# A decoder block with routed experts on one core: the rows of the attention operands are filled straight from SBUF tiles instead of through DRAM

## The chip, the core and the metric

The kernel runs on one core of a Trainium2 chip. The metric is the device time of one execution in microseconds (us). Three runs of the kernel before gave 652.01, 650.23 and 651.17 us, a median of 651.17 us.

## The reference, cut to what matters

The inputs are `x` and `ctx`, both of 32 sequences x 128 tokens x 128 features in float32. There are 16 heads of 8 features each.

```
x = layernorm(x + attn(x, x, causal), ln1)
x = layernorm(x + attn(x, ctx), ln2)
x = layernorm(x + moe(x), ln3)            # 8 experts, 128 -> 512 -> 128, the two best of each token
attn: Q, K, V = linear maps; scores = Q K^T / sqrt(8) by head; softmax; times V; output map
```

## The kernel before, in words

**Tiles and stages.** The 32 sequences go through in 8 groups of 4 (`G = 4`). Each group has a self-attention item ("s") and a cross-attention item ("c"), taken in the order s0, s1, s2, c0, s3, c1 and so on. An s item has 3 steps and a c item 4, so there are 56 steps. In each step TensorE computes scores with queries on the partitions (`scores_q`), VectorE takes each query's maximum (`maximum`, L995), and 3 steps later TensorE computes the same scores with keys on the partitions (`scores_k`), now with the maximum subtracted, and ScalarE takes the exponential (L1448). After the attention of all groups the tokens go through the experts in 71 blocks (L1680 to L1772).

**How a score is computed.** The products are in bfloat16, and an fp32 value is the sum of three bfloat16 parts. `parts` (L856) makes them for the queries ("q") or keys ("k") of one item, 32 times in all: one projection on TensorE (L788) gives 128 features x 512 tokens; ScalarE rounds it to part 1 (L864); VectorE takes the remainder (L868); GpSimd rounds that to part 2 (L872) and takes what is left as part 3 (L875); for the first queries VectorE does these two. The parts lie in a tile `p3`, of which there are 3. The operand of the scores is another tile `at` (`qk` in the profile; 3 for queries, 3 for keys): partition `8a + t` holds, for eight column blocks i (one for each pair of heads), term t of one feature. Terms 0 to 5 are six products of parts (`terms`), so that one matmul over 64 partitions sums them. On the query side, terms 6 and 7 carry the negated maximum, as a high and a low bfloat16 part; on the key side these rows hold a constant selector, `sel`.

**How the rows are filled.** The rows of `at` mix features of all heads, so the parts go through DRAM. The whole `p3` is stored to a DRAM tile `pd` (L885, 384 KB; for the first queries and keys part by part, L880), and six transfers of 128 KB read it back in the order that `at` wants (L901). On the query side the rows of the maximum must be zero while `scores_q` runs: when a query tile is used again, two transfers copy zeros from a DRAM tile `zero_d` (L896).

**How the maxima reach their rows.** `transposed_maxima` (L998) splits the maxima on GpSimd into high and low parts (L1008, L1009), transposes them on TensorE (L1016), copies them out on ScalarE (L1023) into `nmT` with 32 partitions, and two transfers spread the 16 high and the 16 low rows into rows 6 and 7 of each eight (L1029).

**What sets the order.** `Plan` (L172) simulates the engines and queues by listed durations, latencies and priorities, and writes out one fixed order for each engine; buffers are given out by the same simulation, from the first task that names a buffer until the last one that names it has ended. On the chip each engine and queue runs its list in order and waits by semaphores. SP's queue issues nearly all transfers, ACT's queue some weights and the rows of the first keys. The rows of an item may not be filled earlier than 5 steps ahead of its first step (`LEAD`, L1413 to L1415).

Of the kernel before, what the change touches and what calls it, by code (L numbers as in the profile page):

```python
# [10 lines left out]
BF16 = mybir.dt.bfloat16  # L11
# [6 lines left out]
P = 128  # L18
H = 16
HD = 8  # L20
E = 8
# [315 lines left out]
def kernel(  # L337
# [67 lines left out]
    sel = sb([P, 8], "sel")  # L405
    zero_d = dram.tile([16, 8, G * P], BF16, name="zero_d")
    maskq = sb([P, HALF], "maskq", BF16)
# [73 lines left out]
    def c_sel():  # L481

        nc.vector.tensor_scalar(ti[:, 2:3], ti[:, 0:1], 7, None, ALU.bitwise_and)
        nc.vector.tensor_scalar(ti[:, 3:4], ti[:, 0:1], 56, None, ALU.bitwise_and)
        nc.vector.tensor_copy(tf[:, 0:2], ti[:, 2:4])
        nc.vector.tensor_scalar(tf[:, 0:1], tf[:, 0:1], 6.0, ONES16, ALU.is_ge, ALU.mult)
        nc.vector.tensor_scalar(tf[:, 2:10], tf[:, 64:72], 8.0, None, ALU.mult)
        nc.vector.tensor_scalar(sel, tf[:, 2:10], tf[:, 1:2], tf[:, 0:1], ALU.is_equal, ALU.mult)
# [44 lines left out]
    def colsrc(src):  # L533
        return src.rearrange("(p o) -> p o", o=1)

    raw = {}
    t_raw = {}
    for n, w, prio, q in (
        ("wqs", sa_wq, -30, "ACT"), ("wks", sa_wk, -29, "ACT"), ("wvs", sa_wv, -26, "ACT"), ("wkc", ca_wk, -12, "SP"),
        ("wos", sa_wo, -16, "SP"), ("wvc", ca_wv, -11, "SP"), ("wqc", ca_wq, -13, "SP"), ("woc", ca_wo, -5, "SP"),  # L540
    ):
        raw[n] = spare[:, 0:P] if n == "wqc" else sb([P, P], n)
        t_raw[n] = load(raw[n], w, prio, q)
# [3 lines left out]
    for n, src, prio, q in (  # L547
        ("bqs", sa_bq, -28, "ACT"), ("bks", sa_bk, -27, "ACT"), ("bvs", sa_bv, -15.5, "SP"), ("g1", ln1_g, -12.9, "SP"),
        ("b1", ln1_b, -12.8, "SP"), ("bqc", ca_bq, -12.7, "SP"), ("bkc", ca_bk, -11.9, "SP"), ("bvc", ca_bv, -5, "SP"),
        ("g2", ln2_g, 0, "SP"), ("b2", ln2_b, 0, "SP"),  # L550
    ):
        cols[n] = sb([P, 1], "col_" + n)
        t_col[n] = load(cols[n], colsrc(src), prio, q)
    rws = {}
    t_row = {}
    for i, (n, src, w) in enumerate((
# [8 lines left out]

    wp = {n: raw[n] for n in ("wqs", "wks", "wkc")}
    t_wp = {n: t_raw[n] for n in wp}
    wp["wqc"] = sb([P, P], "wqcp")
    t_wqc = t_wp["wqc"] = early(
        "DVE", 0.3, -5, lambda: nc.vector.tensor_scalar(wp["wqc"], raw["wqc"], cols["g1"], None, ALU.mult),  # L570
        [t_raw["wqc"], t_col["g1"]],
    )
    bqc = sb([P, 1], "bqc")

    def pe(dur, prio, fn, deps, bufs, mode="128x128"):
# [3 lines left out]
    t = pe(  # L579
        0.3, -4, lambda b=b_q: nc.tensor.matmul(b.at[:, 0:1], lhsT=raw["wqc"], rhs=cols["b1"], start=True, stop=True),  # L580
        [t_raw["wqc"], t_col["b1"]], [b_q],
    )
# [207 lines left out]
    def prepare(kind, gi):  # L790
# [13 lines left out]
        def copied(b=bank):  # L804
# [10 lines left out]
        it.K, it.t_K, it.t_pK = parts(  # L815
            wp["wk" + n], cols["bk" + n], xT, [t, t_wp["wk" + n], t_col["bk" + n]], t0 - 4.45, (1, 2, 1, 2, 3, 1), f"k{kind}{gi}"
        )
# [38 lines left out]
    def parts(w, b, xT, deps, prio, terms, name):  # L856


        bank, p3, r1, at = Buf(s_ps), Buf(s_p3), Buf(s_r1), Buf(s_q if name[0] == "q" else s_kk)
        pd = dram.tile([3, P, G * P], BF16, name="pd_" + name)  # L860
        t1 = pe(1.12, prio, lambda: project(bank.at, w, xT.at), deps, [bank, xT, p3])
# [15 lines left out]
        soon = name in ("qs0", "ks0")  # L877
        if soon:
            t6 = it_store[name] = [
                add("SP", 0.5, -24 + 0.1 * k, lambda k=k: nc.sync.dma_start(out=pd[k], in_=p3.at[:, k, :]), [t_], [p3], lat=2.4)  # L880
                for k, t_ in enumerate((t2, t4, t5))
            ]
        else:
# [5 lines left out]
        q = "ACT" if name == "ks0" else "SP"  # L889
        dq = nc.scalar if q == "ACT" else nc.sync  # L890
# [7 lines left out]
        for t, k in enumerate(terms):  # L898

            def rows(t=t, k=k):  # L900
                dq.dma_start(out=at.at[t::8], in_=pd[k - 1].rearrange("(i a) n -> a i n", i=8))  # L901

            t7.append(
                add(q, 0.66 if q == "SP" else 0.85, (-23 + 0.1 * k if soon else prio + 0.37) + 0.01 * t, rows, [t6[k - 1], *cleared], [at], lat=3.6)
            )
        return at, t7, t5
# [91 lines left out]
    def transposed_maxima(tl, ti_, nm, deps):  # L998
# [5 lines left out]
        def split():  # L1004
            src = nm.at[:, 0 : 16 * two].rearrange("p (h j r a) -> p a j h r", h=2, j=2, r=4)
            for a in range(two):
                top, low = [nmx.at[:, a, k].rearrange("p j (h r) -> p j h r", h=2) for k in range(2)]
                nc.gpsimd.tensor_copy(top, src[:, a])  # L1008
                nc.gpsimd.tensor_tensor(low, src[:, a], top, ALU.subtract)  # L1009
# [3 lines left out]
        def tr():  # L1013
            b16 = bank.at.bitcast(BF16)
            for a in range(two):
                nc.tensor.transpose(  # L1016
                    b16[0:32, a * P : (a + 1) * P], nmx.at[:, a].rearrange("p k j c -> p (k j c)"), ident16
                )
# [7 lines left out]
        def spread():  # L1026
            c0 = P * tl[2] if tl[0] == "c" else 0 if two == 2 else 2 * P + P * tl[2]
            for k in range(2):
                nc.sync.dma_start(  # L1029
                    out=it.Q.at[6 + k :: 8, :, c0 : c0 + P * two],  # L1030
                    in_=bc(nmT.at[16 * k : 16 * k + 16, 0 : P * two], 1, 8),
                )

        it.nmt[tl] = add("SP", 1.3, ti_ - 18.37, spread, [t], [nmT, it.Q], lat=3.2)

# [838 lines left out]
```

## Time and profile before

| | us |
|---|---|
| median of three runs | 651.17 (650.23 to 652.01) |
| profiled execution, its own time | 654.44 |
| its span in the profile | 652.4 |
| PE (TensorE matmuls) busy | 481.2 (74%) |
| DVE (VectorE) busy | 360.5 (55%) |
| POOL (GpSimd) busy | 331.8 (51%) |
| ACT (ScalarE) busy | 315.0 (48%) |

The span is the time from the first to the last instruction that the profile shows; 654.44 - 652.4 = 2.0 us lie around it. The shares are averages over stages that differ: the filling of the pipeline, the steps of attention, and the expert blocks. The transfers moved 100.07 MB, a mean of 153 GB/s.

### The profile page before, as it was taken

Reading aid. Unit: us, or ns where it says so; the run is one execution under the profiler, and the core shown is the slowest. Engines: PE = TensorE matmul, PEld = TensorE weight load, DVE = VectorE, ACT = ScalarE, POOL = GpSimd, SP = SyncE. Lnnn points to the kernel's source line nnn. Section 1 sums busy time; section 2 is a strip of 40 time slices with the busy share of each in tenths; the row PEclk is TensorE's granted clock in tenths of the full one; section 3 lists DMA queues with packets and bytes.
Section 4 is the critical chain, followed back from the end, with each engine's and each line's share of the span. In section 5 each row is a group of like instructions: output and inputs, shape, how many; then the busy total and the mean of one; then the engine's idle time right before and its main releaser. Section 6 shows DMA issues by size and latency. Waiting matters only on the chain.

```text
span 652.4 us, 23363 instructions
## 1 busy us (share of the span) xinstructions
PE 481.2 (74%) x8571; PEld 370.6 (57%) x8571; DVE 360.5 (55%) x995; ACT 315.0 (48%) x719; POOL 331.8 (51%) x570
## 2 busy tenths in 40 slices
PE   6557688887788788898787845678848899696760
PEld 4234465564655554656565723577748788586750
DVE  5477436766678576786748747113602224635527
ACT  3214254565455654556563532545525567565630
POOL 4623114452357457367583765445365334657473
PEclk9567779988899989899899865689968999987975
DMA  5566776546664654745442134344448657665422
GB/s 156 123 203 174 200 201 181 174 146 199 173 168 118 191 153 136 210 122 168 145 147 87 32 110 118 103 137 137 133 136 246 182 173 229 191 191 153 150 76 64
DMA packets 118719, 100.07 MB, mean 153 GB/s; under 512 B 25931, under 2 KB 105967, under 8 KB 118144
## 3 DMA queue, kind: packets, MB, share of 16 engines
q1 hardware_dynamic: 107888, 84.69, 45.5%
q0 software_dynamic: 4320, 8.47, 3.8%
q10 hardware_dynamic: 6400, 5.45, 2.8%
q8 instruction: 69, 1.13, 0.8%
q14 instruction: 42, 0.34, 0.2%
HBM read 68.39 MB, written 26.42 MB: 145 GB/s over the span
## 4 chain that ended last, share of the span: by engine, by line
PE 37%; DVE 16%; issue 13%; POOL 9%; SPq 8%; DMA 8%; ACT 4%; another core or an unknown queue 3%; DVEq 1%; ACTq 0%; POOLq 0%
PE ps L935 12%; PE ps L1723 8%; PE ps L1745 8%; DVE nm L995 6%; SPq L901 4%; DMA qk<-nmT 3%; PE ps L788 2%; SPq L1029 2%; ACT pr L1448 2%; DVE y L1802 2%; POOL rs L1141 1%; PE ps L1705 1%; PE ps L782 1%; POOL res_d L1767 1%
## 5 line engine op out<-in xcount | busy, mean ns | idle before, releaser
L995 DVE TENSOR_REDUCE nm<-ps 128x8 f32<-128x1024 f32 (+1 forms) x112 | 133.1, 1219 | 43.9 <-PE ps L935 35.8
L1448 ACT ACTIVATE pr<-ps 128x1024 f32<-128x1024 f32 x112 | 110.9, 1023 | 86.6 <-PE ps L935 75.2
L935 PE MATMUL ps<-qk,qk 64*64 64x128 bf16 (+2 forms) x3072 | 99.1, 228 | 49.5 <-DVE nm L995 12.0
L935 PEld LDWEIGHTS <-qk 64*64 64x64 bf16 (+1 forms) x3072 | 66.3, 113 | 90.8 <-issue 36.4
L1767 POOL DMA_INDIRECT res_d<-o,id x71 | 70.0, 985 | 82.3 <-DVE o L1762 37.6
L1336 POOL DMA_INDIRECT rows_d<-y,rid x64 | 64.9, 1014 | 40.9 <-issue 17.2
L935 PE MATMUL ps<-pr,v 64*32 64x64 f32 (+2 forms) x3072 | 77.7, 277 | 7.4 <-issue 7.2
L935 PEld LDWEIGHTS ps<-pr,v 64*32 64x32 f32 (+1 forms) x3072 | 61.2, 115 | 24.1 <-issue 17.4
L1745 PE MATMUL ps<-wall,qk 128*128 x336 | 50.4, 298 | 18.6 <-ACT qk L1737 10.2
L1737 ACT ACTIVATE qk<-ps,b1c 128x128 f32<-128x128 f32 x168 | 48.1, 378 | 28.9 <-PE ps L1723 17.7
L1745 PEld LDWEIGHTS ps<-wall,qk 128*128 128x128 f32 x336 | 44.5, 207 | 23.4 <-ACT qk L1737 11.9
L1008 POOL CAST nmx<-nm 128x16 bf16<-128x16 f32 x64 | 12.6, 196 | 82.5 <-DVE nm L995 81.9
L1723 PE MATMUL ps<-bx,qk 128*128 128x128 f32 x336 | 47.7, 290 | 3.8 <-ACT bx L1710 3.8
L1737 ACT ACTIVATE k<-ps,b1c 128x128 f32<-128x128 f32 x116 | 33.2, 378 | 30.9 <-PE ps L1705 9.2
L1755 DVE TENSOR_SCALAR id<-xT,tab_e 128x1 int32<-128x1 f32 x47 | 12.8, 273 | 62.5 <-SPq L1640 28.8
L1723 PEld LDWEIGHTS ps<-bx,qk 128*128 128x128 f32 x336 | 44.1, 205 | 4.6 <-ACT bx L1710 4.0
L1095 DVE STREAM_TRANSPOSE u<-ps 128x512 f32<-128x512 f32 x32 | 21.8, 701 | 41.6 <-PE ps L935 40.5
L1762 DVE TENSOR_TENSOR o<-ps,b2r 128x128 f32<-128x128 f32 x71 | 20.1, 290 | 43.9 <-PE ps L1745 23.1
L1723 PE MATMUL ps<-bx,w 128*128 128x128 f32 x232 | 35.6, 306 | 10.6 <-ACT bx L1710 8.5
L1710 ACT ACTIVATE bx<-ps,col_b,col_g 128x128 f32<-128x128 f32 x71 | 33.0, 473 | 19.2 <-remote 9.2
L1723 PEld LDWEIGHTS ps<-bx,w 128*128 128x128 f32 x232 | 32.6, 217 | 12.1 <-ACT bx L1710 9.2
L1168 ACT ACTIVATE y<-y,rs 128x128 f32<-128x128 f32 x58 | 25.0, 491 | 29.8 <-POOL rs L1142 29.8
(269 smaller groups left out, 888.5 us busy)
## 6 DMA issues: line engine op xcount, KB each, us to landing
qk<-in_L_xattn_e_w_dram SPq DMA_DIRECT2D x42, 256.0 KB
w<-in_L_xattn_e_w_dram SPq DMA_DIRECT2D x29, 256.0 KB
qk<-pd_qs SPq DMA_DIRECT2D x48, 128.0 KB
qk<-pd_kc SPq DMA_DIRECT2D x48, 128.0 KB
qk<-pd_qc SPq DMA_DIRECT2D x48, 128.0 KB
qk<-pd_ks SPq DMA_DIRECT2D x42, 128.0 KB
qk<-zero_d SPq DMA_DIRECT2D x28, 128.0 KB
pr<-res_d ACTq DMA_DIRECT2D x7, 512.0 KB
```

Of the source, the lines that this page charges most:

```text
L901: dq.dma_start(out=at.at[t::8], in_=pd[k - 1].rearrange("(i a) n -> a i n", i=8))
L935: nc.tensor.matmul(out_, lhsT=lhsT, rhs=rhs, start=start, stop=stop, skip_group_check=True)
L995: lambda: nc.vector.tensor_reduce(dst(), src(), AX.X, ALU.max, negate=True), [dep], [pair, nm, turn],
L1095: t = add("DVE", dve(512), prio, lambda: nc.vector.transpose(u1.at, bank.at), [dep], [bank, u1])
L1168: lambda i=i: nc.scalar.activation(dst(i), src(i), AF.Identity, bias=rs.at[:, 1, i : i + 1], scale=rs.at[:, 0, i : i + 1],),
L1336: nc.gpsimd.indirect_dma_start(out=rows_d[:, :], out_offset=bass.IndirectOffsetOnAxis(ap=rid.at[:, i, k : k + 1], axis=0), in_=y.at[:, i, ...
L1448: lambda kp=kp, prb=prb, h=h: nc.scalar.activation(prb.at[:, 8 * h : 8 * h + 8, :].rearrange("p h q -> p (h q)"), kp.at.rearrange("p b n - ...
L1710: lambda: nc.scalar.activation(xT.at[:, 0:P], bt.at[:, 0:P], AF.Identity, bias=cols["b2"], scale=cols["g2"]),
L1723: nc.tensor.matmul(p1.at[:, c * P : (c + 1) * P], lhsT=w1.at[:, c, :], rhs=xT.at[:, 0:P], start=True, stop=True)
L1737: nc.scalar.activation(h.at[:, c, :], p1.at[:, c * P : (c + 1) * P], AF.Gelu, bias=b1c[:, bass.ds(w["act"] + c, 1)],)
L1745: nc.tensor.matmul(p2.at[:, 0:P], lhsT=h.at[:, c, :], rhs=flat[:, bass.ds(w["pe"] + c * P, P)], start=c == 0, stop=c == NFC - 1,)
L1767: nc.gpsimd.indirect_dma_start(out=res_d[:, :], out_offset=bass.IndirectOffsetOnAxis(ap=idb.at[:, 0:1], axis=0), in_=o.at, in_offset=None, ...
```

## The change: what it does

Three edits belong together.

1. The columns of the query and key weights (and the biases) are permuted once, so that feature 8a + i of a projection is what feature 16i + a was. Then the eight partitions 8a to 8a + 7 of a part are the eight column blocks of row a, and `at.at[t::8]` can be filled by one transfer from `p3.at[:, k, :]`, SBUF to SBUF. The stores to `pd` and the tile `pd` go. A row's transfer waits for its own part alone. `p3` is now named by the row transfers, so it is held until they have landed. The permutation is four VectorE copies of 128x128 float32; the raw weights lie in the memory of expert 5's second matrix until then.
2. The two rows of the maximum are terms 3 and 7 in place of 6 and 7. The high and low parts alternate in `nmx`, so that one transfer spreads all 32 rows of `nmT` to `at[3::4]`.
3. For the same reason one transfer of zeros to `at[3::4]` takes the place of two; `zero_d` has 32 rows of 8 KB.

The listed latency of a row transfer is 2.6 where it was 3.6, that of the spread 2.4 where it was 3.2. The loads that may not overtake the first fill (`begun`) wait in the plan for the row transfers instead of the stores.

```diff
+    for n, prio in (("wqs", -29.5), ("wks", -28.5), ("wkc", -5.1), ("wqc", -5.2)):
+        t_wp[n] = permuted(n, prio)      # early("DVE", 0.3, prio, tensor_copy(out_, byhead(raw[n])))
...
-            wp["wk" + n], cols["bk" + n], xT, [...], t0 - 4.45, (1, 2, 1, 2, 3, 1), f"k{kind}{gi}"
+            wp["wk" + n], cols["bk" + n], xT, [...], t0 - 4.45, (3, 2, 1, 0, 1, 2, 1, 0), f"k{kind}{gi}"
...
-            wp["wq" + n], b, xT, [t_xT, t_wp["wq" + n], t_b], prio, (1, 1, 2, 2, 1, 3), f"q{n}{gi}"
+            wp["wq" + n], b, xT, [t_xT, t_wp["wq" + n], t_b], prio, (1, 1, 1, 0, 2, 2, 3, 0), f"q{n}{gi}"
...
-        pd = dram.tile([3, P, G * P], BF16, name="pd_" + name)
...
-            t6 = [add(
-                "SP", 0.6, prio + -1.05, lambda: nc.sync.dma_start(out=pd.rearrange("k p n -> p k n"), in_=p3.at), [t5], [p3], lat=2.8
-            )] * 3
...
-        for t in (6, 7) if again else ():
-                add(q, 0.66, prio + 0.4, lambda t=t, dq=dq: dq.dma_start(out=at.at[t::8], in_=zero_d), [t4, t_zero, *cleared], [at], lat=3.0)
+        if again:
+                    q, 0.6, prio + 0.4,
+                    lambda: dq.dma_start(out=at.at[3::4].rearrange("a i n -> a (i n)"), in_=zero_d), [t4, t_zero, *cleared],
...
-                dq.dma_start(out=at.at[t::8], in_=pd[k - 1].rearrange("(i a) n -> a i n", i=8))
-                add(q, 0.66 ..., (-23 + 0.1 * k if soon else prio + 0.37) + 0.01 * t, rows, [t6[k - 1], *cleared], [at], lat=3.6)
+                    dq.dma_start(out=at.at[t::8], in_=p3.at[:, k, :])
+                    add(q, 0.6, (-23 + 0.1 * k if soon else prio + 0.37) + 0.01 * t, rows, [t_, *cleared], [p3, at], lat=2.6)
+                if soon:
+                    it_store.setdefault(name, []).append(t7[-1])
...
-            for k in range(2):
-                nc.sync.dma_start(
-                    out=it.Q.at[6 + k :: 8, :, c0 : c0 + P * two],
-                    in_=bc(nmT.at[16 * k : 16 * k + 16, 0 : P * two], 1, 8),
-                )
-        it.nmt[tl] = add("SP", 1.3, ti_ - 18.37, spread, [t], [nmT, it.Q], lat=3.2)
+            nc.sync.dma_start(out=it.Q.at[3::4, :, c0 : c0 + P * two], in_=bc(nmT.at[:, 0 : P * two], 1, 8))
+        it.nmt[tl] = add("SP", 0.65, ti_ - 18.37, spread, [t], [nmT, it.Q], lat=2.4)
```

## Rows read from the trace of the kernel before

**Rows 1.** Busy time of each engine (with its number of instructions), the granted TensorE clock as a share of full speed, the mean busy share of the 16 DMA engines and GB/s, in five stretches of the span.

```profile
0.00:30.00 30.00, 17.98 (x174) 10.40 (x174) 14.38 (x37) 9.08 (x14) 17.99 (x41) 0.81 0.58 147
30.00:60.00 30.00, 17.56 (x362) 9.86 (x362) 24.02 (x50) 7.29 (x11) 6.33 (x18) 0.63 0.60 173
...
210.00:240.00 30.00, 23.24 (x649) 16.69 (x649) 19.95 (x58) 17.42 (x30) 16.25 (x32) 0.94 0.71 202
360.00:400.00 40.00, 24.32 (x283) 17.71 (x283) 27.57 (x114) 13.67 (x31) 24.81 (x50) 0.71 0.30 90
...
420.00:652.00 232.00, 168.22 (x1289) 156.46 (x1289) 90.78 (x344) 119.36 (x390) 119.68 (x143) 0.88 0.54 158
```

**Rows 2.** The chain of work that ended last, over the whole span, by engine ("SPq" is SP issuing transfers, "DMA" a transfer under way).

```profile
PE 37%; DVE 16%; issue 13%; POOL 9%; SPq 8%; DMA 8%; ACT 4%; another core or an unknown queue 3%; DVEq 1%; ACTq 0%; POOLq 0%
```

**Rows 3.** What PE waited for from 60 to 385 us: total us, times, longest.

```profile
PE ps L935 <- issue: 17.0, 19, 4.2
PE ps L935 <- DMA qk<-nmT: 8.8, 6, 2.8
PE ps L935 <- DVE nm L995: 6.4, 15, 0.9
PE ps L935 <- ACT pr L1448: 6.2, 12, 1.0
...
PE ps L935 <- DMA qk<-pd_kc: 4.1, 2, 2.1
...
PE ps L788 <- DMA pd_kc<-p: 1.1, 1, 1.1
```

**Rows 4.** SP's queue from 207 to 240 us in order of time: start, us until the last issue of the piece has ended, line, transfer, number of issues.

```profile
207.74 0.38 SPq L885 DMA_DIRECT2D pd_qc<-p  x1
...
208.81 0.51 SPq L885 DMA_DIRECT2D pd_kc<-p  x1
...
210.68 1.22 SPq L901 DMA_DIRECT2D qk<-pd_qc  x2
211.99 1.21 SPq L1029 DMA_DIRECT2D qk<-nmT  x2
213.25 3.56 SPq L901 DMA_DIRECT2D qk<-pd_qc  x4
216.86 5.24 SPq L901 DMA_DIRECT2D qk<-pd_kc  x6
...
230.23 4.90 SPq L901 DMA_DIRECT2D qk<-pd_ks  x6
...
236.70 2.51 SPq L1029 DMA_DIRECT2D qk<-nmT  x4
```

**Rows 5.** Transfers that stand in the chain of waits, in order of time: start, us from issue to landing, transfer.

```profile
69.41 5.24 DMA qk<-nmT
...
117.84 2.70 DMA qk<-pd_qc
...
155.69 3.36 DMA pd_kc<-p
...
272.41 3.29 DMA qk<-pd_qs
...
402.42 1.92 DMA qk<-nmT
```

**Rows 6.** The start, all engines in order of time: start, us, engine, line, operation, tiles, number; in brackets the idle time before and what ended it.

```profile
9.20 0.69 ACT L864 ACTIVATE p<-ps,col_bqs 128x512 bf16<-128x512 f32 x1 [0.17 <-PE ps L788]
...
12.04 0.69 DVE L875 TENSOR_TENSOR p<-u,p 128x512 bf16<-128x512 f32 x1
...
14.15 6.23 ACTq L901 DMA_DIRECT2D qk<-pd_ks  x4
...
14.43 6.76 SPq L901 DMA_DIRECT2D qk<-pd_qs  x6
...
24.39 0.64 PE L935 MATMUL ps<-qk,qk 64*64 64x64 bf16 x32 [0.29 <-DMA wall<-in_L_xattn_sa_bo_dram]
```

**Rows 7.** The last cross item (c7), from 376 us, in the same columns.

```profile
376.15 0.68 ACT L864 ACTIVATE p<-ps,bqc 128x512 bf16<-128x512 f32 x1
...
379.20 1.16 POOL L875 TENSOR_TENSOR p<-u,p 128x512 bf16<-128x512 f32 x1
...
380.39 0.52 SPq L885 DMA_DIRECT2D pd_qc<-p  x1
...
383.41 3.78 SPq L901 DMA_DIRECT2D qk<-pd_qc  x6
...
390.56 1.04 PE L935 MATMUL ps<-qk,qk 64*128 64x128 bf16 x16
...
394.28 4.61 DVE L995 TENSOR_REDUCE nm<-ps 128x8 f32<-128x1024 f32 x4
...
401.25 5.04 SPq L1029 DMA_DIRECT2D qk<-nmT  x6
```

**Rows 8.** What SP's queue itself waited for, over the span: total us, times, longest.

```profile
SPq L1029 <- ACT nmT L1023: 29.8, 14, 5.3
...
SPq L896 <- POOL p L872: 9.0, 4, 4.4
```

**Rows 9.** A float32 operation of VectorE on 128x128 elements, from the chain of waits: start, us, line.

```profile
28.91 0.29 DVE wall L599
```

More of the change, by code (lines that the diff above doesn't have):

```diff
@@ L405 @@
     sel = sb([P, 8], "sel")
-    zero_d = dram.tile([16, 8, G * P], BF16, name="zero_d")
+    zero_d = dram.tile([32, 8 * G * P], BF16, name="zero_d")
     maskq = sb([P, HALF], "maskq", BF16)
@@ L552 @@
         cols[n] = sb([P, 1], "col_" + n)
-        t_col[n] = load(cols[n], colsrc(src), prio, q)
+        by_ = src.rearrange("(i a o) -> a i o", i=8, o=1) if n in ("bqs", "bks", "bqc", "bkc") else colsrc(src)
+        t_col[n] = load(cols[n], by_, prio, q)
     rws = {}
@@ L563, with permuted @@
     t_rw = load(rw, router_w, 0.5)
[L566 to L568 removed]
+    wp, t_wp = {}, {}
+    wqcr = spare[:, 7 * P : 8 * P]
+    def permuted(n, prio):
+        wp[n] = sb([P, P], n + "p")
+        out_ = wp[n].rearrange("p (a i) -> p a i", i=8)
+        if n == "wqc":
+            out_ = wqcr.rearrange("p (a i) -> p a i", i=8)
+        return early("DVE", 0.3, prio, lambda: nc.vector.tensor_copy(out_, byhead(raw[n])), [t_raw[n]])
+    for n, prio in (("wqs", -29.5), ("wks", -28.5), ("wkc", -5.1), ("wqc", -5.2)):
+        t_wp[n] = permuted(n, prio)
+    t_wqcr = t_wp["wqc"]
     t_wqc = t_wp["wqc"] = early(
[L570 to L571 removed]
+        "DVE", 0.3, -5, lambda: nc.vector.tensor_scalar(wp["wqc"], wqcr, cols["g1"], None, ALU.mult), [t_wqcr, t_col["g1"]]
     )
@@ L877, in parts @@
         soon = name in ("qs0", "ks0")
[L878 to L883, printed above, removed]
-            t6 = [add(
-                "SP", 0.6, prio + -1.05, lambda: nc.sync.dma_start(out=pd.rearrange("k p n -> p k n"), in_=p3.at), [t5], [p3], lat=2.8
-            )] * 3
         again = name[0] == "q" and name not in ("qs0", "qs1")
-        q = "ACT" if name == "ks0" else "SP"
-        dq = nc.scalar if q == "ACT" else nc.sync
+        q, dq = ("ACT", nc.scalar) if name == "ks0" else ("SP", nc.sync)
         n = 1 if name[1:] == "s0" else 2 if name[1:] == "s1" else 3
@@ L893, in parts, with rows @@
         t7 = []
-        for t in (6, 7) if again else ():
+        if again:
             t7.append(
-                add(q, 0.66, prio + 0.4, lambda t=t, dq=dq: dq.dma_start(out=at.at[t::8], in_=zero_d), [t4, t_zero, *cleared], [at], lat=3.0)
-            )
-        for t, k in enumerate(terms):
-            def rows(t=t, k=k):
-                dq.dma_start(out=at.at[t::8], in_=pd[k - 1].rearrange("(i a) n -> a i n", i=8))
-            t7.append(
-                add(q, 0.66 if q == "SP" else 0.85, (-23 + 0.1 * k if soon else prio + 0.37) + 0.01 * t, rows, [t6[k - 1], *cleared], [at], lat=3.6)
-            )
+                add(
+                    q, 0.6, prio + 0.4,
+                    lambda: dq.dma_start(out=at.at[3::4].rearrange("a i n -> a (i n)"), in_=zero_d), [t4, t_zero, *cleared],
+                    [at], lat=3.0,
+                )
+            )
+        for k, t_ in enumerate((t2, t4, t5)):
+            for t in range(8):
+                if terms[t] != k + 1:
+                    continue
+                def rows(t=t, k=k):
+                    dq.dma_start(out=at.at[t::8], in_=p3.at[:, k, :])
+                t7.append(
+                    add(q, 0.6, (-23 + 0.1 * k if soon else prio + 0.37) + 0.01 * t, rows, [t_, *cleared], [p3, at], lat=2.6)
+                )
+                if soon:
+                    it_store.setdefault(name, []).append(t7[-1])
         return at, t7, t5
@@ L1006, in split @@
             for a in range(two):
-                top, low = [nmx.at[:, a, k].rearrange("p j (h r) -> p j h r", h=2) for k in range(2)]
+                top, low = [nmx.at[:, a, :, :, k].rearrange("p j (h r) -> p j h r", h=2) for k in range(2)]
                 nc.gpsimd.tensor_copy(top, src[:, a])
```

26 lines of the change are left out of this document (16 added, 10 removed).

## The prediction

> **What bounds the kernel now.** I read the busy times by stretch first [rows 1]. From 0 to 60 us no engine is full except VectorE from 30 to 60 (24.0 of 30 us): the pipeline is filling. In a stretch of the steps of attention, 210 to 240, PE is busy 23.2 of 30 us at a granted clock of 0.94, the other engines 16 to 20. From 360 to 400 PE falls to 24.3 of 40, because the last cross item waits for a long serial chain. The expert blocks from 420 on, 232 us, touch nothing that the change touches: they start when attention ends and can only be shifted.
>
> The chain of work that ended last [rows 2] gives PE 37%, and SP's queue and transfers 8% each, some 104 us of 652 together. A chain is one path: when a step in it shortens, the next one behind it takes over. So I asked PE itself what it waited for in the steps [rows 3]: transfers into the operand tiles 8.8 + 4.1, a store 1.1, together 14.0 us; VectorE's maxima 6.4 and exponentials 6.2 stand right beside them, and 17.0 us are not explained.
>
> SP's queue in order of time [rows 4] shows why transfers are late: from 207.7 to 239.2 us it hardly pauses. The rows of qc3 are issued at 210.7, 2.9 us after their store at 207.7; those of kc3 at 216.9, 8.1 us after their store; spreads of maxima stand between and behind them. Rows of a six that should take 6 x 0.60 = 3.6 us take 5.24, so the queue also waits inside.
>
> **The change, part by part.**
>
> *Issues removed.* 32 stores (30 whole, 2 in three pieces) are 36 issues, 14 second clearings, 56 second spreads: 106 issues. At 0.38 to 0.61 us each [rows 4], 0.55 as the middle, that is 58 us of SP's queue, in about 380 us of attention. The 192 row transfers stay. The clearing keeps its bytes, 32 runs of 8 KB in place of 256 of 1 KB; the spread keeps 256 runs in one transfer. I cost both at the price of one issue, since a store of 384 runs issues in 0.38 to 0.51 us, no more than a row transfer of 128 (0.60) [rows 4].
>
> *How soon a row from SBUF lands.* The trace has row transfers from DRAM (2.70 and 3.29 us from issue) and spreads, which go from SBUF to SBUF: 1.92 when the queue is quiet, 5.24 when it is crowded [rows 5]. Bounds are thus 1.9 and 5.2. I take 3.0, the middle of the DRAM rows: a row moves four times the bytes of most spreads to the very partitions of today's rows. On this the Trainium skill ("DMA: Bandwidth & Descriptors", section on the anatomy of one DMA) says that most of the fixed cost is the receipt from the memory written to, which stays SBUF; by that rule nothing is gained at this point, and no row of the kernel before separates it from the other reading. By the quiet spread it would be 3.0 - 1.9 = 1.1 us at each serial place; the sum goes by 3.0, with no gain.
>
> *The start.* Today the first query part 3 is ready at 12.04 + 0.69 = 12.73. Then come a store and the rows; SP's last row is issued by 14.43 + 6.76 = 21.19 and the first score starts at 24.39, 3.20 later [rows 6]. After: SP can issue from 9.20 + 0.69 = 9.89, when ScalarE's part is ready, six rows of 0.60; the sixth waits for part 3 at 12.73 and ends by 13.35; score at 13.35 + 3.20 = 16.55. That is 7.8 us earlier. But six rows took 6.76 us instead of 3.6: 3.2 us of waiting for earlier transfers, among them a load of x that stays. With that kept, the gain is 4.7; I take 5. Bounds: 3.0 (a store's leg alone, the 3.36 us less some waiting) and 7.8. Added here are the permuting copies: four of 0.29 us if like a VectorE operation on the same 128x128 float32 [rows 9], twice that if the strided read costs. Two lie before the first projection, beside the transposes of x; if that cover is gone they cost 0.3 to 1.2. Two fall into the stretch where VectorE is nearly full: 0.6 to 1.2. I charge 0.6 in all.
>
> *The tail.* c7 is serial: part 3 ends at 379.20 + 1.16 = 380.36, the store is issued at 380.39, the rows from 383.41 to 387.19, the first score starts at 390.56, 3.37 later [rows 7]. After: five rows go out while GpSimd still works on part 3, the sixth is issued at 380.4 to 381.0, the score starts at 384.3. That is 6.2 earlier. At 401.25 six spread issues take 5.04 us [rows 7]; three remain, and I credit 1.0, one issue and some waiting. VectorE's first maximum of c7 is only at 394.28, 3.7 us after the first score, since routing work for c6 stands there; part of the gain meets it, so I take off 1.2 and book 6.0. Bounds: 3.0 (the store's leg, 380.39 to 383.41, alone) and 8.3 (6.2, 1.0, and 1.1 for quicker landing).
>
> *The steps between.* At most the 14.0 us of [rows 3] can go. VectorE's maxima and the exponentials are late next, 12.6 us in the same table, so I book under half, 6. Bounds 0 and 14; the 17.0 without a cause are not counted.
>
> *What is added.* A row now waits for its part from ScalarE or GpSimd in SP's queue, with spreads behind it. SP waits so already: 9.0 us for GpSimd's part at the clearing, 29.8 for the copy of the maxima [rows 8]; the store waited for the last part as well, so I cost the exchange at nothing, hidden in queue time that is freed. `p3` is held longer. PE's one wait for a store, at a projection, is just such a hold: 1.1 [rows 3]. Store landing was 208.81 + 3.36 = 212.2 for kc3, the last row's about 222.1 + 2.4 = 224.5: a hold of 12 us more, less what the earlier issue gives back. I charge 2.0, twice the wait seen; bounds 0 and 20 (below). One plan for all engines is worked out anew, with other durations; a shift of either sign comes with that, which I put at 3 us either way, one of the longer PE waits (up to 4.2 [rows 3]).
>
> *Sum.* 5 + 6 + 6 - 0.6 - 2.0 = 14.4 us. Against the profiled execution: 654.44 - 14.4 = 640.0. That execution stands 3.3 above the median of 651.17, so for the median 636.8.
>
> **The rivals.**
>
> *Only the two ends gain.* In the steps PE is at 78% and goes straight from waiting for a transfer to waiting for maxima; SP's freed time is then cover that nobody needed. For it: 6.4 + 6.2 us of other waits, already as long as those for transfers. Against: PE stands up to 2.8 us at once for a spread [rows 3]. Gain 5 + 6 - 2.6 = 8.4, time 642.8.
>
> *Rows from SBUF land slowly.* If reading and writing SBUF at once makes each row land like the crowded spread, 5.2 instead of 3.0, the start and tail lose 2.2 each and the steps gain nothing: 8.4 - 4.4 = 4.0, time 647. Against it: 1.92 for the last spread.
>
> *`p3` is held until its rows have landed (slower).* The place is the projection: 32 operands in turn share three tiles, and a projection that finds none free stands at the head of PE's queue, scores behind it. The row may not be filled until the target tile is free, so an operand made early blocks a third of the supply. If in each of the 7 later groups the query projection and the key projection wait as long as PE's longest wait for a spread, 2.8 us [rows 3], that is 39 us; with half of them, 20 us. The latter, against 5 + 6 + 6 - 0.6 = 16.4 of gains, gives 651.2 + 3.6 = 655. It decides once more than six such waits come. Against it: rows that start as soon as part 1 is there end about when the store ended, where the target is free, as it was for qc3, which had been cleared before the store landed [rows 4].
>
> *No change* (the gains all given back by the new plan): 650 to 652.
>
> **How the numbers follow.** Chances: forecast 0.50, ends only 0.22, slow rows 0.07, held `p3` 0.13, no change 0.08. A measurement of this kernel tells about 0.3% from no change, 2 us. Faster by more than that: 0.50 + 0.22 + most of 0.07 = 0.78; within: 0.08; slower: 0.14. The predicted time is 636.8. All upper bounds together, 7.8 + 14 + 8.3 = 30, give 621; the range begins at 620. At the top it takes in the ends-only case, slow rows and no change, and leaves the greater part of the held `p3`: 653.
>
> **What would show each step.** First score at 16 to 20 us instead of 24.4, and no `pd` transfers at all. SP with 106 fewer issues and gaps in the stretch that is full now. The first score of c7 3 to 6 us after its last part, instead of 10.2. PE's waits for transfers in the steps under 8 us, with waits for maxima and exponentials grown. Slow rows would show in the chain as row transfers of over 4 us; held tiles as PE waiting before L788 for a row transfer. I am wrong if the steps from 100 to 360 us take as long as before or longer although SP is relieved, or if the tail stays at 10 us because the plan puts other work ahead of it.

## The result and the profile after

| | before | after |
|---|---|---|
| median of the runs, us | 651.04 (650.23 to 652.01, 4 runs) | 633.41 (630.55 to 636.41, 4 runs) |
| span in the profile, us | 652.4 | 634.7 |
| PE, DVE, POOL, ACT busy, us | 481.2, 360.5, 331.8, 315.0 | 483.2, 362.1, 332.9, 314.5 |
| moved by transfers, MB | 100.07 | 87.63 |

The ratio is 0.9729, with a 95% interval of 0.9682 to 0.9776: faster by 17.6 us. 636.8 (620 to 653) was predicted, so the direction and the size were right. Several terms inside the sum were not, and most of what follows is about them.

The engines work as long as before, so all of the gain is waiting. Busy time by stretch, as in [rows 1]: stretch, its length, PE, PE's weight loads, DVE, ACT, POOL, clock, DMA share, GB/s (the last stretch begins at 405, since the experts start earlier):

```profile
0.00:30.00 30.00, 19.90 (x240) 11.88 (x240) 16.83 (x42) 9.58 (x15) 14.99 (x38) 0.89 0.66 151
30.00:60.00 30.00, 16.27 (x324) 8.57 (x322) 21.67 (x51) 9.84 (x15) 10.41 (x25) 0.71 0.75 179
210.00:240.00 30.00, 24.06 (x549) 16.31 (x548) 23.32 (x37) 16.46 (x27) 20.07 (x34) 1.00 0.46 124
360.00:400.00 40.00, 30.26 (x439) 22.19 (x435) 29.25 (x112) 19.41 (x37) 22.06 (x47) 0.76 0.31 83
405.00:634.00 229.00, 166.39 (x1270) 153.77 (x1269) 92.41 (x342) 115.74 (x382) 127.76 (x152) 0.89 0.56 161
```

From 210 to 240 the DMA engines are at 0.46 where they were at 0.71, and from 360 to 400 PE works 30.3 us where it worked 24.3. From 30 to 60, still the filling of the pipeline, PE works less than before: 16.3 for 17.6.

SP's queue from 206 to 240, as in [rows 4]. No stores are left, the spreads stand alone, and there are gaps (231 to 237 has two issues):

```profile
206.59 2.56 SPq L915 DMA_DIRECT2D qk<-p  x4
210.36 0.66 SPq L1044 DMA_DIRECT2D qk<-nmT  x1
211.12 1.84 SPq L915 DMA_DIRECT2D qk<-p  x3
213.01 1.04 SPq L905 DMA_DIRECT2D qk<-zero_d  x1
...
225.98 2.11 SPq L915 DMA_DIRECT2D qk<-p  x3
232.18 1.94 SPq L1044 DMA_DIRECT2D qk<-nmT  x2
237.77 0.56 SPq L1370 DMA_DIRECT2D x<-y  x1
```

What SP's queue waited for itself, over the span, as in [rows 8]. A spread is now mostly at the head of the queue before its maxima are there (61.6 us for 29.8), and rows wait for their part:

```profile
SPq L1044 <- ACT nmT L1039: 61.6, 24, 8.3
SPq L915 <- ACT p L882: 32.1, 8, 11.5
```

What PE waited for from 60 to 385, as in [rows 3]:

```profile
PE ps L951 <- issue: 15.5, 20, 2.8
PE ps L951 <- DMA qk<-p: 9.9, 4, 3.6
PE ps L951 <- DVE nm L1011: 6.4, 13, 1.1
PE ps L951 <- ACT pr L1460: 5.5, 11, 1.3
...
PE ps L951 <- DMA qk<-nmT: 3.5, 5, 1.2
```

Waits for spreads fell from 8.8 to 3.5; those for rows rose from 5.3 (4.1 in [rows 3], and 1.2 in two smaller lines) to 9.9. Together that is 13.4 for 14.1, so PE waits for transfers nearly as long as before.

The start, as in [rows 6]:

```profile
9.49 0.69 ACT L882 ACTIVATE p<-ps,col_bqs 128x512 bf16<-128x512 f32 x1 [0.35 <-PE ps L807]
...
10.20 4.24 SPq L915 DMA_DIRECT2D qk<-p  x6
...
12.16 0.69 DVE L893 TENSOR_TENSOR p<-u,p 128x512 bf16<-128x512 f32 x1
```

PE from there, in the same columns:

```profile
18.77 2.05 PE L807 MATMUL ps<-xT,wksp 128*128 128x512 f32 x2 [0.67 <-DMA qk<-p]
20.74 0.64 PE L951 MATMUL ps<-qk,qk 64*64 64x64 bf16 x32
...
34.84 2.04 PE L807 MATMUL ps<-xT,wksp 128*128 128x512 f32 x2 [3.31 <-DMA rw<-in_L_xattn_router_w_dram]
```

Six rows are issued in 4.24 us in place of 6.76, and the first score starts at 20.74 for 24.39. In the third line the bracket names a small load, but that is only the transfer that came last on one semaphore. The semaphores on which this projection waits are those of the six row transfers issued at 24.96 to 28.19, the last of which landed at 34.49. It waits for a `p3` tile.

This wait is not new. In before the same projection waited at the same place, for the store of its `p3` tile; that store was issued at 29.70 and landed at 34.54. The lines of before, and that of the later trace f1 of the same kernel, where the bracket names the store:

```profile
29.70 0.38 SPq L885 DMA_DIRECT2D pd_qs<-p  x1
...
34.67 2.04 PE L788 MATMUL ps<-xT,wks 128*128 128x512 f32 x2 [3.53 <-POOL nmx L1008]
```

```profile
33.55 2.05 PE L788 MATMUL ps<-xT,wks 128*128 128x512 f32 x2 [3.07 <-DMA pd_qs<-p]
```

The last cross item, as in [rows 7]:

```profile
369.88 0.69 ACT L882 ACTIVATE p<-ps,bqc 128x512 bf16<-128x512 f32 x1 [1.48 <-PE ps L807]
...
370.59 1.88 SPq L915 DMA_DIRECT2D qk<-p  x3
...
372.35 1.18 POOL L1362 TENSOR_TENSOR y<-y,row_g 128x512 f32<-128x512 f32 x1
...
373.17 1.23 SPq L915 DMA_DIRECT2D qk<-p  x2
...
373.60 1.18 POOL L1363 TENSOR_TENSOR y<-y,row_b 128x512 f32<-128x512 f32 x1
...
374.74 1.16 POOL L893 TENSOR_TENSOR p<-u,p 128x512 bf16<-128x512 f32 x1
...
375.92 0.54 SPq L915 DMA_DIRECT2D qk<-p  x1
```

The rows of part 1 are in the queue 0.02 us after ScalarE has written it. The first score of c7 starts at 378.58, 2.7 us after the last part ended (10.2 before), and its first maximum at 379.23.

### The profile page after: what moved, and what is told of

It reads as the page before. It is cut to its first block, busy times and chain, and to the rows that moved or that the text cites. A ratio compares the mean times of both kernels' runs of the same rounds, so it can differ in the third digit from the quotient of the medians.

```text
span 634.7 us, 23395 instructions
## 1 busy us (share of the span) xinstructions
PE 483.2 (76%) x8571; PEld 372.8 (59%) x8571; DVE 362.1 (57%) x999; ACT 314.5 (50%) x719; POOL 332.9 (52%) x570
## 2 busy tenths in 40 slices
DMA packets 104753, 87.63 MB, mean 138 GB/s; under 512 B 24235, under 2 KB 91983, under 8 KB 104160
## 4 chain that ended last, share of the span: by engine, by line
PE 40%; DMA 14%; DVE 12%; issue 11%; SPq 6%; ACT 6%; POOL 5%; another core or an unknown queue 3%; ACTq 1%; DVEq 1%; POOLq 0%
PE ps L951 14%; PE ps L1757 7%; PE ps L1735 6%; DMA qk<-p 5%; DVE nm L1011 4%; SPq L915 3%; DMA qk<-nmT 3%; PE ps L807 3%; ACT pr L1460 2%; PE ps L801 2%; DMA res_d<-o,id 2%; DVE y L1814 2%; ACT qk L1749 1%; PE ps L843 1%
## 5 line engine op out<-in xcount | busy, mean ns | idle before, releaser
L951 PE MATMUL ps<-qk,qk 64*64 64x64 bf16 (+2 forms) x3072 | 97.5, 227 | 43.2 <-DMA qk<-p 9.9
L951 PEld LDWEIGHTS <-qk 64*64 64x64 bf16 (+1 forms) x3072 | 66.3, 112 | 86.5 <-issue 41.7
L1757 PE MATMUL ps<-wall,k 128*128 x232 | 35.8, 303 | 19.1 <-ACT k L1749 18.5
L1735 PE MATMUL ps<-bx,qk 128*128 128x128 f32 x336 | 46.1, 284 | 2.7 <-ACT bx L1722 2.7
L1774 DVE TENSOR_TENSOR o<-ps,b2r 128x128 f32<-128x128 f32 x71 | 20.6, 291 | 43.5 <-PE ps L1757 20.2
L1735 PEld LDWEIGHTS ps<-bx,qk 128*128 128x128 f32 x336 | 42.4, 198 | 3.7 <-ACT bx L1722 2.9
L1757 PEld LDWEIGHTS ps<-wall,k 128*128 128x128 f32 x232 | 31.6, 211 | 21.8 <-ACT k L1749 21.1
L1180 ACT ACTIVATE y<-y,rs 128x128 f32<-128x128 f32 x58 | 24.7, 485 | 29.8 <-POOL rs L1154 29.8
L1722 ACT ACTIVATE bx<-ps,col_b,col_g 128x128 f32<-128x128 f32 x71 | 33.1, 470 | 11.6 <-PE ps L1717 4.4
L893 POOL TENSOR_TENSOR p<-u,p 128x512 bf16<-128x512 f32 x31 | 35.8, 1156 | 1.8
```

Of the source, the lines that this page charges most:

```text
L893: lambda: eng.tensor_tensor(p3.at[:, 2, :], r1.at, p3.at[:, 1, :], ALU.subtract), [t4], [p3, r1],
L951: nc.tensor.matmul(out_, lhsT=lhsT, rhs=rhs, start=start, stop=stop, skip_group_check=True)
L1180: lambda i=i: nc.scalar.activation(dst(i), src(i), AF.Identity, bias=rs.at[:, 1, i : i + 1], scale=rs.at[:, 0, i : i + 1],),
L1722: lambda: nc.scalar.activation(xT.at[:, 0:P], bt.at[:, 0:P], AF.Identity, bias=cols["b2"], scale=cols["g2"]),
L1735: nc.tensor.matmul(p1.at[:, c * P : (c + 1) * P], lhsT=w1.at[:, c, :], rhs=xT.at[:, 0:P], start=True, stop=True)
L1757: nc.tensor.matmul(p2.at[:, 0:P], lhsT=h.at[:, c, :], rhs=flat[:, bass.ds(w["pe"] + c * P, P)], start=c == 0, stop=c == NFC - 1,)
```

## Where the time went, by maxima

The 112 maxima on VectorE, counted in the order in which they start, give a clock through the attention. Their items differ a little between two plans. Each number is the start of that maximum in the trace. The first two columns are the kernels above; the next four come from one later series (below), where before has a span of 632.9.

| maximum | before | after | before (f1) | after (f2) | f3 | f4 |
|---|---|---|---|---|---|---|
| 1 | 26.3 | 21.9 | 26.2 | 21.1 | 26.1 | 20.2 |
| 7 | 47.5 | 49.7 | 46.6 | 49.2 | 47.0 | 41.7 |
| 16 | 73.9 | 74.4 | 73.4 | 73.6 | 73.9 | 74.3 |
| 22 | 109.8 | 103.2 | 108.0 | 99.7 | 105.1 | 97.9 |
| 49 | 185.9 | 171.9 | 186.2 | 170.6 | 175.2 | 171.7 |
| 103 | 355.6 | 350.6 | 355.1 | 345.2 | 338.3 | 338.9 |
| 112 | 402.2 | 387.8 | 401.8 | 380.5 | 385.0 | 376.0 |
| span | 652.4 | 634.7 | 632.9 | 609.2 | 616.7 | 613.4 |

After gains 4.4 at the start, has lost them by the seventh maximum (2.2 behind), is 14.0 ahead by the 49th, 5.0 at the 103rd, and 14.4 at the last one; the rest, 3.3, comes behind it. Each column is one execution: the two traces of before differ by at most 1.8 in these rows, the two of after by up to 7.3 (at the last maximum).

## The experiments

The twelve runs were measured in three series, e, f and g ("calls" in the expectations). In these the kernel before took 633.9, 632.3 and 655.4 us, so ratios are set beside each other (95% intervals in brackets). The ratio of the whole change is itself 0.9729 in the comparison above and 0.9638 in f, so a difference of 0.9% between two series says little; after itself did not run in e and g.

### One half at a time

**e1_one_spread_same_plan**: before, with one spread and one clearing (edits 2 and 3); rows still through DRAM.

```diff
-            for k in range(2):
-                nc.sync.dma_start(out=it.Q.at[6 + k :: 8, ...], in_=bc(nmT.at[16 * k : 16 * k + 16, ...], 1, 8))
+            nc.sync.dma_start(out=it.Q.at[3::4, ...], in_=bc(nmT.at[:, ...], 1, 8))
...
-        for t in (6, 7) if again else ():   # add(q, 0.66, ..., at.at[t::8] <- zero_d, ...)
+        if again:                           # add(q, 1.32, ..., at.at[3::4] <- zero_d, ...)
```

> The kernel before with one spread of the maxima and one clearing in place of two each, and the plan told of the old durations, so that every queue keeps its order: 70 issues fewer on SP, rows still through DRAM. If freed issues of SP's queue are worth time in the steps: 3 to 5 us faster than before (ratio 0.992 to 0.995). If only the row path at the two ends gains: within 0.3% of before. If the new order of the plan is what gains: within 0.3%.

**e2_one_spread**: the same, with the durations that after lists (0.65 and 2.4 for a spread, 0.6 for a clearing).

> The same edit with the plan told of it (0.65 us and 2.4 us latency for the spread, 0.6 for the clearing). Freed issues: 3 to 6 us faster than before. Only the ends: within 0.3%. If the plan's order is what counts: several us away from the run with the old plan, either way.

**e3_rows_only**: edit 1 alone; after with two spreads and two clearings, listed as in before.

```diff
-            nc.sync.dma_start(out=it.Q.at[3::4, ...], in_=bc(nmT.at[:, ...], 1, 8))
+            for k in range(2):
+                nc.sync.dma_start(out=it.Q.at[3 + 4 * k :: 8, ...], in_=bc(nmT.at[k::2, ...], 1, 8))
...
-        it.nmt[tl] = add("SP", 0.65, ti_ - 18.37, spread, [t], [nmT, it.Q], lat=2.4)
+        it.nmt[tl] = add("SP", 1.3, ti_ - 18.37, spread, [t], [nmT, it.Q], lat=3.2)
```

> The changed kernel with two spreads and two clearings again, the plan told of them; rows still straight from SBUF. If the row path makes the gain at the start and the tail: 10 to 13 us faster than before (0.980 to 0.985), the rest being the freed issues. If the ends are all: as fast as the changed kernel (0.973).

**e4_two_issues**: the same two issues for each spread and clearing, but the plan keeps after's numbers, so every engine keeps the order of after.

> The changed kernel in its own order, but each spread and each clearing issued as two transfers: 70 issues put back on SP, nothing else moved. Freed issues worth time: 3 to 5 us slower than the changed kernel (0.978 to 0.981 of before). Only the ends, or the order of the plan: as fast as the changed kernel (0.973).

| | ratio |
|---|---|
| e1 | 0.9682 [0.9622, 0.9743] |
| e2 | 0.9721 [0.9665, 0.9777] |
| e3 | 0.9696 [0.9612, 0.9781] |
| e4 | 0.9887 [0.9844, 0.9931] |

I had expected 3 to 6 us from e1 and e2, 10 to 13 from e3, and 3 to 5 us of loss in e4. By the ratios e1, e2 and e3 gain 20.2, 17.7 and 19.3 us: each gives about as much as the whole change. 70 issues put back into after's order take more than half of it away. So in a given order a freed issue is worth far more than I booked, and the halves do not add.

e3 and e4 have the same transfers and differ by the plan alone: e3's plan is told of the two issues, e4's is not. They ran in one series, and they are 1.9% apart, 613.5 and 626.5 us, with intervals that do not meet. PE's waits for rows from 60 to 385, first e3, then e4:

```profile
PE ps L954 <- DMA qk<-nmT: 10.5, 6, 4.2
...
PE ps L954 <- DMA qk<-p: 7.3, 4, 3.4
```

```profile
PE ps L954 <- DMA qk<-p: 24.0, 7, 6.0
...
PE ps L954 <- DMA qk<-nmT: 6.2, 6, 2.1
```

So what e4 loses is not the price of 70 issues in general, but their price in an order that was made without them. With a plan that knows of them (e3) no loss is shown: 0.9696, where after had 0.9729 and 0.9638.

One correction to what was expected of e1: its clearing is one task where before has two, the plan was made anew with that, and its order is not the order of before. What its order does can be seen at c7:

```profile
341.00 0.69 ACT L864 ACTIVATE p<-ps,bqc 128x512 bf16<-128x512 f32 x1 [2.04 <-PE ps L788]
341.77 1.22 DVE L996 TENSOR_REDUCE nm<-ps 128x8 f32<-128x1024 f32 x1 [0.19 <-PE ps L936]
...
350.60 1.86 SPq L902 DMA_DIRECT2D qk<-pd_qc  x3
...
360.00 1.23 DVE L996 TENSOR_REDUCE nm<-ps 128x8 f32<-128x1024 f32 x1 [0.81 <-PE ps L936]
```

The path from ScalarE's part to the first maximum of c7 is as slow as in before, 19.0 us (18.1 there), since the rows still go through DRAM. But it begins while the maxima of c6 are still being taken. From the last maximum of c6 to the first of c7 it is 12.6 us, against 37.0 in before and 27.1 in after. That comes from the order of the new plan, not from the transfers that edits 2 and 3 take away: f3 below has the same transfers in the order of before, and keeps the 37.0.

### What the issues alone are worth

**f1_before_again** and **f2_after_again** are the two kernels themselves, for traces on one chip.

> The kernel before itself, for its trace beside the other three of this call. Ratio 1.000. If the steps of the maxima and the exponentials differ from the trace shown first by more than the whole span does, the profile of one chip can't be laid beside that of another.

> The kernel after itself, beside the others of this call. If the ratio of the whole change doesn't hang on the chip: 0.973, within 0.968 to 0.978. If it does, something between 0.955 and 0.985, and all comparisons with the earlier call stand under that.

f1 took 634.99 in its one run. f2 came to 0.9638 [0.9561, 0.9715]. The interval overlaps that of the first comparison; the gain of the whole change is 2.7% there and 3.6% here. The spans of f1 and before differ by 19.5 us, nearly all of it behind the last maximum, so that their stretches of attention can be laid side by side.

**f3_exact_order**: e1's instructions, with the plan told of two clearings as before, of which the second issues nothing. Nothing moves on any engine; SP has 70 DMAs fewer.

```diff
+            if not t.ins:        # emit(): a step that issues nothing stands for the one before it
+                t.ins = last
+                continue
...
         for t in (6, 7) if again else ():
-            ... dq.dma_start(out=at.at[t::8], in_=zero_d)
+            ... t == 6 and dq.dma_start(out=at.at[3::4]..., in_=zero_d)
```

> Kernel before with one clearing and one spread in place of two, where the plan still sees two (the second is a step that issues nothing): every engine has its instructions in exactly the order of before, and SP has 70 DMAs fewer. It shows what the issues alone are worth. Theory that SP's queue is the limit: 70 issues put back into the order of after cost 1.6%, so taking them out of the order of before gives 0.984 (10 us), within 0.980 to 0.988; the 0.968 of e1, whose plan was made anew with one step less, is then half a better order. If e1's gain was the issues alone: 0.968. If the order was all of it: 0.993 to 0.997, by the 6 us that the prediction had for half of the issues.

0.9816 [0.9752, 0.9880], as the theory of SP's queue had it. That is 11.6 us of 632.3, for 70 issues, and the order can have no part in it. In the table above, f3 gains 16.8 us between the first maximum and the 103rd, and nothing after that. (The traced pair overstates the gain: its spans are 16.2 apart, the medians of the runs 12.0.) PE's waits from 60 to 385, first f1, then f3:

```profile
PE ps L935 <- DMA qk<-nmT: 15.0, 6, 5.1
PE ps L935 <- issue: 14.5, 16, 3.4
PE ps L935 <- DVE nm L995: 5.5, 12, 0.7
```

```profile
PE ps L940 <- issue: 14.6, 11, 4.4
PE ps L1021 <- POOL nmx L1014: 8.9, 12, 1.7
PE ps L940 <- DVE nm L1000: 8.8, 19, 1.0
...
PE ps L940 <- DMA qk<-nmT: 5.8, 3, 2.5
```

The wait for spreads falls by 9.2 us, and PE then waits for what makes the maxima (GpSimd's split, VectorE's maximum). The size of the fall is rough: the other trace of before has 8.8 for the 15.0 ([rows 3]).

**g3_small_issues**: f3 with a transfer of 128 bytes into a place of its own in DRAM where the second spread or clearing was. Nobody waits for it.

```diff
+    def small(dq):
+        dq.dma_start(out=small_d[n_ : n_ + 1, :], in_=id64[0:1, :])
```

> f3 (order of before, one spread and one clearing) with a transfer of 128 bytes into an own place of DRAM at each place where the second one was, for which nobody waits: SP issues as often as before, but moves less and nobody waits for a second landing. If the time on SP to issue is what the 70 were worth: 0.993 to 1.000, the 0.982 of f3 is gone. If it is the bytes or the wait for a second landing: 0.978 to 0.986. In between, both.

0.9898 [0.9854, 0.9942]. Against 0.9816 for f3, SP's time to issue accounts for about half of what the 70 were worth, 0.8 of 1.8%; the two intervals overlap and are from two series, so the share is rough. The small issues are also shorter, 0.45 us, where half a spread took 0.59 in before, so the whole of the issuing time was not put back. The rest is not bytes: f1, f3 and g3 moved 100.07, 100.19 and 100.20 MB, since one spread carries what the two halves carried. It may be the wait for a second landing or the rest of the issuing time, which this run does not tell apart.

A sign of the mechanism is one number of each trace: how long after ScalarE's copy of the maxima (`nmT`) has ended its spread is issued. This is the mean over the steps from 60 to 360 us, pairing the copies with the spreads in order:

| | before | f1 | f3 | g3 | e1 | e2 | e3 | e4 | after | f2 | g4 |
|---|---|---|---|---|---|---|---|---|---|---|---|
| copy to issue, us | 1.67 | 1.86 | 0.83 | 1.20 | 0.78 | 1.61 | 1.50 | 1.34 | 0.68 | 0.70 | 0.97 |

In the order of before a spread is issued 1.0 us sooner on the mean (f1 to f3), and the small issues bring 0.4 of it back. In the order of after the same holds (f2, e4). It is not all that matters: e2 and e3 gain 3% with 1.61 and 1.50. In e2 the second transfer, which came 0.6 us behind the first, is gone; e3's gain lies at the start and the tail as well.

### The stores

**g4_idle_stores**: after in its own order, with each part's store put back ahead of its last row. Nobody reads it. As built, the scores wait for its landing too, since it stands in one step with that row.

```diff
                 def rows(t=t, k=k):
+                    if k == 2:
+                        dq.dma_start(out=pd.rearrange("k p n -> p k n"), in_=p3.at)
                     dq.dma_start(out=at.at[t::8], in_=p3.at[:, k, :])
```

> Kernel after in its own order, with the 32 stores put back ahead of each last row; nobody reads them. If an issue on SP costs what it cost in e4 (70 for 1.6%): 32 cost 0.7%, so 0.971 to 0.980. If the 12.6 MB that the stores move count beside it: 0.980 to 0.990. If the store cost by its landing alone, for which nobody waits here: 0.962 to 0.973, as after.

1.0018 [0.9986, 1.0050]: the whole gain is gone, far outside what any of the three readings gave. PE's waits from 60 to 360:

```profile
PE ps L954 <- DMA qk<-p: 16.6, 6, 5.7
PE ps L954 <- issue: 15.6, 22, 3.0
```

The rows' waits are 16.6 us (7.3 in after, same stretch). The row behind the store is issued half a microsecond later and the store lands later than the row: at c7 the row is issued by 390.53 and the first score starts at 393.70, 3.2 us later, against 378.58 - 376.46 = 2.1 in after. But the c7 path as a whole, from ScalarE's part to the first maximum, is 10.7 us for 9.4, and the loss is in the steps: the 103rd maximum starts at 365.6, 350.6 in after. So 32 stores in an order made without them cost the whole gain, though no row is read from DRAM. Issue, bytes and landing are not told apart by this run, and neither is the order: as with e4, the plan was not told of them, and e3 beside e4 shows that this alone can cost 1.9%.

### The hold of p3

**f4_four_p3**: after with a fourth `p3` tile, in memory that one of the three tiles of the experts' first weights and two of the four `o` tiles share. The loads of those weights wait besides for the last inputs of the attention, and the plan is made anew.

```diff
-    s_p3 = Slots(places(3, [P, 3, G * P], "p3", BF16))
+    s_p3 = Slots([*places(3, [P, 3, G * P], "p3", BF16), shared.bitcast(BF16).rearrange("p (k n) -> p k n", k=3)])
```

> Kernel after with a fourth p3 tile, made of places that the experts' weights and two o tiles share. Theory that the hold of p3 until its rows have landed takes back a part of the gain: the halves gave 0.968 and 0.970 alone, 0.938 if they added up; with a fourth tile 0.945 to 0.962, and TensorE's waits before the projection for a row transfer are gone. Theory that both halves relieve the same queue and nothing is held: 0.970 to 0.977, TensorE waits as before. If the new plan decides: anything from 0.96 to 0.985, with waits moved elsewhere.

0.9655 [0.9593, 0.9717], f2 0.9638. The total does not move, but the path does. PE's two waits for `p3` before a projection from 15 to 62 us, in f2, and then its longest wait in that stretch, which is for a spread (4.48 us at 43.53 in after):

```profile
18.02 1.99 PE L807 MATMUL ps<-xT,wksp 128*128 128x512 f32 x2 [1.73 <-DMA qk<-p]
...
33.17 2.05 PE L807 MATMUL ps<-xT,wksp 128*128 128x512 f32 x2 [2.44 <-DMA col_b<-in_L_xattn_ln_b_dram]
...
43.12 0.64 PE L951 MATMUL ps<-qk,qk 64*64 64x128 bf16 x16 [5.73 <-DMA qk<-nmT]
```

and all that is left of those before a projection in f4:

```profile
32.60 2.05 PE L808 MATMUL ps<-xT,wkcp 128*128 128x512 f32 x2 [0.89 <-DMA qk<-p]
```

So the hold is real, but it is not shown to eat the gain of the start. Before had such waits too: 0.43 and 3.07 us in f1, together 3.5 for the 4.2 of f2. And by the 16th maximum f4, which hardly holds PE, is as late as f1 and f2 (74.3, 73.4 and 73.6), though it was 7.5 us ahead of f2 at the seventh. At the last maximum it is 4.5 ahead, less than the two traces of after differ by. What takes the gain of the start away stays open. In the total f4's lead is gone: from the first expert block to the last, f4 takes 199.7 us, f2 192.8 and f1 194.4. The shared memory is not needed to explain that: e1 (199.2) and e3 (200.4), which also end their maxima early (368.5 and 373.0), lose as much there without it, while f3 (194.6) and e2 (192.7) lose nothing. What in the experts' stage takes 6 us back was not tried.

### The plan

**g1_plan_a** and **g2_plan_b**: after with its instructions unchanged; only listed durations differ, so the order does.

```diff
 # g1
-    ... rows ... lat=2.6      # spread lat=2.4, clearing 0.6
+    ... rows ... lat=3.2      # spread lat=3.2, clearing 1.0
 # g2
-        it.nmt[tl] = add("SP", 0.65, ti_ - 18.37, spread, [t], [nmT, it.Q], lat=2.4)
+        it.nmt[tl] = add("SP", 1.0, ti_ - 18.37, spread, [t], [nmT, it.Q], lat=2.4)
```

> Kernel after with its instructions unchanged; only the numbers that the plan is told of rows, spread and clearing differ (rows land after 3.2 in place of 2.6, spread 3.2 in place of 2.4, clearing 1.0 in place of 0.6), so every engine's order is another. Theory that the order of the new plan is worth as much as the instructions: more than 0.8% from after (0.973 and 0.964 in two calls), here to the good side, 0.945 to 0.960, with c7's query parts made earlier. Theory that the order is worth little and the instructions all: 0.962 to 0.975.

> Kernel after with its instructions unchanged; the plan is told that a spread takes SP 1.0 us in place of 0.65. Theory that the order is worth as much as the instructions: 0.978 to 0.995, well above g1, so that the same instructions lie 2% or more apart. Theory that the instructions decide: 0.962 to 0.975, as g1.

0.9599 [0.9530, 0.9668] and 0.9651 [0.9575, 0.9728]. The 2% that I expected between them did not come; the intervals overlap, and both lie beside f2 (0.9638). For after, no worth of the order alone is shown here: the ratios are half a per cent apart, the medians 6.0 us. It can be worth more: e3 and e4, within one series, differ by the plan alone and are 1.9% apart; e1 and f3 have the same transfers as well, 0.9682 and 0.9816, in two series. g1 is the lowest ratio of all that ran, but not shown to be faster than after.

## Why the prediction was right, and where it was not

- **What bounds it.** Right: no engine, but waits, with SP's queue as a resource whose relief gains time. f3 shows it without a change of order.
- **Start, 5 booked.** The first score came 3.65 us earlier, inside the bounds of 3.0 to 7.8, but at 20.74, not at 16 to 20. The six rows took 4.24 us to issue, where 3.6 was the least. I had looked at SP's rows alone: the last row of the first keys, on ACT's queue, was issued at 14.90 and landed at 19.82.
- **Landing of a row, 3.0 kept.** Right. From the end of the issue to landing, from 60 to 380 us, the medians are 2.37 to 2.67 from DRAM in before and 2.39 from SBUF in after. By the rule of the Trainium skill ("DMA: Bandwidth & Descriptors", anatomy of one DMA, a section on transfers issued from GpSimd), that the fixed cost is mostly the receipt from the memory written to, a new source would gain nothing, and these medians agree. The quiet spread's price, 1.1 us less at each place, does not come.
- **`p3` held, 2.0 charged.** Not borne out as a price of the change. I read PE's waits from 60 us on and took the one of 1.1 for the only one of its kind. Before 60 us the kernel before waited for `p3` too, 0.58 and 3.53 us, and after waits 0.67 and 3.31. PE waiting for rows before a projection, the sign that I had named, is there, but together the two waits are 4.0 us where they were 4.1 for the stores (4.2 and 3.5 in f2 and f1); the rival's 20 us did not come.
- **The steps, 6 booked of 14.** They did not come where I booked them. From the 22nd maximum to the 103rd, some 100 to 355 us, before takes 245.8 us and after 247.4 (f1 247.1, f2 245.5): as long as before, which I had named as a sign of being wrong. PE's waits for transfers, which I had under 8 us, are 13.4. Two steps failed. I put at nothing that rows now wait for their part in SP's queue; SP stands 32.1 us for ScalarE's part there over the span, and PE's waits for rows rose by 4.6 while those for spreads fell by 5.3. And I took PE's own waits for a transfer as the measure of what the queue is worth: f3, in the order of before, takes 233.2 us for the same maxima, 13.9 less than f1, with 70 of the 106 issues. A late spread also moves VectorE's and ScalarE's work, and what follows was counted as waits for maxima and "issue"; that last part is argued. After's order does not keep what f3 shows; g1, the same instructions in another order, takes 238.9.
- **Why the halves don't add.** f3, f4 and e3 start the 103rd maximum at 338.3, 338.9 and 338.7. That looks like what the steps have to give before the maxima bind, but it is no such floor: g1 starts it at 332.4. What the traces show is that the order decides as much as the issues (e3 and e4), and that the experts take some 6 us back where the attention ends early in e and f. The rest stays open.
- **The tail, 6.0 booked.** Undersized. From ScalarE's part to the first maximum of c7 it was 18.1 and is 9.4: 8.8 us. The store's leg and the rows behind part 3 are as worked out (14.4 us to the first score, now 8.7; 5.7 for the 6.2). What failed is the 1.2 taken off for VectorE's routing work: that work now lies elsewhere, and the first maximum follows its score after 0.65 us in place of 3.7. f3, with the store left in, keeps the tail as it was (18.1 us). GpSimd's two operations of another group between parts 2 and 3 (L1362 and L1363) hold part 3 up by 2.4 us (372.38 to 374.74).
- **Permuting copies, 0.6.** 0.27 and 0.26 for the first two, while the loads before the first projection land until 6.2 us; nothing waits for them. The third, at 24.14, has 1.73 in its record, but the next maximum starts 0.17 us after it; the fourth has 0.26.
- **Plan, ±3.** Not shown to be wrong for after (g1, g2), but e3 and e4 show that the order can be worth 13 us when the plan is not told what is issued.
- **The sum.** 14.4 against 17.6, and this nearness is partly luck. By the maxima of the first pair, with what was booked in brackets: 4.4 up to the first maximum (5 - 0.6), 0.6 from there to the 103rd (6 - 2.0), 9.4 from there to the last (6), and 3.3 behind it, where nothing was booked. In f1 and f2 it is 5.1, 4.8, 11.4 and 2.4. The wrong signs that I had named (slow rows over 4 us in the chain of waits) do appear in the start, as 4.02 and 6.55 us, and once in the steps, 4.35; not in the tail (2.31).

## What to carry to other kernels

When one queue issues nearly all transfers, count a removed issue by what stands behind it in that queue, and not by the wait of one engine for it: here 70 issues were worth 1.8% without anything else moving. Where a planner fixes the order, tell it of every issue before you judge an edit: the same transfers in two orders lay 1.9% apart (e3, e4). Two edits that relieve the same queue should not be added up; find what is late next. An edit that lets a transfer read a tile directly also makes that tile live longer; look for the wait at the place where the tile is taken again, while the pipeline fills as well, and look there in the kernel before too: here the wait stood there already, for the store.

## What was not expected of the hardware

- A 128-byte transfer holds SP's queue for most of the time of a large one: in g3 the median issue is 0.45 us, against 0.64 us for a spread of 32 x 8 x 128 elements or more, and 0.60 for a row of 128 KB. So fewer transfers relieve the queue, and smaller ones do so much less. The Trainium skill ("DMA: Bandwidth & Descriptors", section "Issuing engines are not separate DMA queues") calls the sequencer's time to start a DMA usually small relative to the DMA itself. Here it is 0.60 against a landing of 2.39, small for one transfer, but the 329 issues of before from 60 to 360 us hold SP for 220 of the 300 us.
- One transfer in place of two lands no later: a whole spread lands 1.93 us after its issue ended in after, one half of a pair 1.96 in before (medians, 60 to 380 us).
- During the filling, six rows of 128 KB in a row landed 5.4 to 6.6 us after their issue began (24.96 to 30.39, 28.19 to 34.49), with weight loads ahead of them in the same queue; in the steps it is 0.60 + 2.39 = 3.0.
